# Making a block of the combined weights by pairs of row chunks with seven block products for eight

## The chip, the cores and the metric

The kernel runs on one core of one Trainium2 chip. The metric is the device time of one execution in microseconds. The core has five engines that run beside each other and meet at semaphores: TensorE (PE in the profile; its weight loads are listed apart as PEld), VectorE (DVE), ScalarE (ACT), GpSimd (POOL) and SyncE (SP), which here only issues DMAs. ScalarE and GpSimd issue DMAs too, and all DMAs run on the same 16 DMA engines.

## What is computed

Two mixture layers are applied to x of 32 batches x 128 tokens x 1024 channels, all in f32. Cut to what matters here:

```
# layer 0: every batch's channels are mixed by its own 128x128 matrix; then 64 experts, 8 per token
h = einsum('bct,bcd->bdt', x, L0_cond_weights[itok_B_1_198])
x = x + moe(h, gate_w, wg, wu, wd)
# layer 1: a linear map with a low-rank adapter per batch, then a base map with routed low-rank experts
H = x @ W.T + ((x @ A[i].T) @ Bm[i].T) * scalings[i]
x = x + (H @ base_w.T + base_b) + lora experts, whose inner maps and router also read H
```

In layer 1 everything that follows H is linear in it up to the router and the inner maps, so the kernel never makes H. It multiplies the weights instead: head = [inner maps of the lora experts (128 columns), router (8 columns), base_w.T (1024 columns)], 1160 columns in all, and the combined weights are W.T @ head (eight chunks of 128 rows) and Bm.T @ head (one chunk of 128 rows, the 8 adapters x 16). These nine row chunks, each a product over 1024 = 8 x 128, are what the change touches. They depend on weights alone, so they can be made at any time before the last stage.

## The kernel before

There are three stages. In the first (lines 344 to 549) a loop over the 32 batches mixes a batch's channels on TensorE (`mixed`, tiles ph), copies the result out on ScalarE (hT), turns it into token rows on VectorE (`as_rows`, hq) and stores it (`stored`, to hbuf); it makes the router's logits (`logits`, plog), takes the best eight of 64 (`topped`), the exponentials on ScalarE (`powers`) and the weights (`weights_of`), and every four batches counts the tokens of each expert (`counted`, tiles pcnt and prk). The second stage (line 578 on) goes through the 64 experts, each with 256 slots; its token rows are gathered by the counts that the first stage leaves. The third (line 882 on) applies layer 1 to pairs of batches.

The head's columns are cut into three blocks (`BLOCKS`, line 38): 0 to 388, 388 to 776, 776 to 1160. The first 136 columns, the inner maps and the router, lie in block 0; block 1 has base-map columns only. A block of one row chunk is made by `combined(n, d)` (line 465): eight matmuls of 128 x 128 by 128 x 388, summed in one PSUM bank (pcw), a ScalarE copy to SBUF (cw) and a store to cwbuf in HBM, from where the third stage reads it. For d = 8, the adapters' chunk, the copy goes to G_sb, which stays in SBUF. Block 0 is made in the first stage, one chunk behind each of batches 8, 11, 14, 17, 20, 23 and 26 and two behind the last; block 1 in the second stage's start, while the first gathers are on their way (line 812); block 2 in the third stage's start.

The left operand of these products, W.T and Bm.T, is loaded in three parts of three row chunks (`left_block`, tiles WB_a, 1.5 MB each): chunks 0 to 2 at batch 2, 3 to 5 at batch 5, 6 to 8 at batch 9. The right operand is one block of the head's columns (`head_block`, tile hw, 1.55 MB), loaded at batch 2 for block 0 and at batch 22 for block 1. The x of batch b + 6 is loaded at batch b into a ring of six buffers (`loaded_batch`). From batch 10 on one batch of x a turn is also copied from HBM to HBM (`carried`, to ybuf).

The order of the work is written out by hand: `dve`, `pe`, `act`, `pool` and `sync` (line 221) wrap the engines so that every instruction keeps its place in the program, and because that helper is at line 219, most rows of the profile carry L219 and are told apart by their tiles. DMAs issued by SP and ScalarE take turns on eight semaphores; an issue whose semaphore is still in use waits for the DMA that had it before to land.

`weight_sums` and `token_sums` (lines 610 and 622), `product` (634) and the same helpers of the later stages are the scheme that the change brings to the first stage as well: seven products of half-sized blocks in place of eight.

Of the kernel before, what the change touches and what calls it, by code (L numbers as in the profile page):

```python
# [8 lines left out]
F32 = mybir.dt.float32  # L9
# [3 lines left out]
ALU = mybir.AluOpType  # L13
# [4 lines left out]
P = 128  # L18
# [3 lines left out]
HC = H // P  # L22
# [15 lines left out]
BLOCKS = [(0, 388), (388, 776), (776, NO)]  # L38
PIECES = [(0, 126), (126, 320), (320, 512)]
BW = 388  # L40
NS = BLOCKS[1][1]
NA = NX + R
HH = HC // 2
# [3 lines left out]
NQ = P // Q  # L47
W4 = H // NQ
# [3 lines left out]
def kernel(  # L52
# [37 lines left out]
    cwbuf = dram.tile([P, HC, NS], F32, name="cwbuf")  # L90
# [86 lines left out]
    fs = fpool.enter_context(tc.tile_pool(name="fs", bufs=1))  # L177
# [10 lines left out]
    def head_block(n):  # L188
        lo, hi = BLOCKS[n]
        hw = wts.tile([P, HC * BW], F32, name=f"hw_{n}", tag="wg")  # L190
        hw = hw[:, 0 : HC * (hi - lo)].rearrange("p (j o) -> p j o", j=HC)
        sync.dma_start(hw, head_w[:, lo:hi].rearrange("(j p) o -> p j o", p=P))
        return hw
# [6 lines left out]
    def multiplied(n, d, hw, left, pool, tag, pe):  # L200
        w = BLOCKS[n][1] - BLOCKS[n][0]
        pcw = pool.tile([P, 512], F32, name=f"pcw_{n}_{d}", tag=tag)[:, 0:w]
        for j in range(HC):
            if j == HC // 2:
                yield
            pe.matmul(pcw, left[d][:, j, :], hw[:, j, :], start=(j == 0), stop=(j == HC - 1))
        yield pcw
# [5 lines left out]
    class InOrder:  # L213
# [7 lines left out]
    dve, pe, act, pool, sync = (  # L221
        InOrder(e) for e in (nc.vector, nc.tensor, nc.scalar, nc.gpsimd, nc.sync)
    )
# [121 lines left out]
    pa_big = ppool.enter_context(tc.tile_pool(name="pa_big", bufs=4, space=PSUM))  # L345
    pa_sm = ppool.enter_context(tc.tile_pool(name="pa_sm", bufs=3, space=PSUM))
    with (
# [6 lines left out]
        def loaded_batch(b):  # L354
            ws[b] = a6.tile([P, P], F32, name=f"w_{b}", tag="w_b")
            pool.indirect_dma_start(
                out=ws[b],
                out_offset=None,
                in_=cond_w,
                in_offset=bass.IndirectOffsetOnAxis(ap=cond_rows[:, b : b + 1], axis=0),  # L360
            )
            xs[b] = a6.tile([P, HC, P], F32, name=f"x_{b}", tag="x_q")
            queue = pool if 2 <= b < 6 else sync
            queue.dma_start(xs[b].rearrange("p j c -> p (j c)"), x_q[b])
# [5 lines left out]
        def mixed(b):  # L370
            hT = a2.tile([P, HC, P], F32, name=f"hT_{b}", tag="hT", bufs=4)
            x_b, w_b = xs.pop(b), ws.pop(b)
            for n in range(2):
                ph = pa_big.tile([P, HH, P], F32, name=f"ph_{b}_{n}", tag="big")
                for j in range(HH):
                    pe.matmul(ph[:, j, :], x_b[:, n * HH + j, :], w_b, start=True, stop=True)
                act.copy(hT[:, n * HH : (n + 1) * HH, :], ph)
            hTs[b] = hT


        def as_rows(b):
            hqs[b] = a2.tile([P, NQ, HC, Q], F32, name=f"hq_{b}", tag="hq", bufs=3)
            dve.transpose(
                hqs[b].rearrange("p b j c -> p j b c"),
                hTs[b].rearrange("p j (b i) -> p j b i", i=Q),
            )

        def stored(b):
            act.dma_start(
                hbuf[b * P : (b + 1) * P, :], hqs.pop(b).rearrange("p b j c -> p (b j c)")  # L390
            )

        def logits(b):
            g, t = divmod(b, GB)
            if t == 0:
                plogs[g] = pa_sm.tile([P, GB, E], F32, name=f"plog_{g}", tag="sm")
            hT = hTs[b]
            for j in range(HC):
                pe.matmul(
                    plogs[g][:, t, :],  # L400
                    hT[:, j, :],
                    gw_sb[:, j, :],
                    start=(j == 0),
                    stop=(j == HC - 1),
                )
# [59 lines left out]
        def combined(n, d):  # L465
            lo, hi = BLOCKS[n]
            halves = multiplied(n, d, hws[n], lefts, pa_big, "big", pe)
            next(halves)
            yield
            pcw = next(halves)  # L470
            if d < HC:
                cw = fs.tile([P, BW], F32, name=f"cw_{n}_{d}", tag="cw", bufs=3)[:, 0 : hi - lo]
                act.copy(cw, pcw)
                act.dma_start(cwbuf[:, d, lo:hi], cw)
            else:
                act.copy(G_sb[:, lo:hi], pcw)
            yield

        loaded_batch(0)
        gw_sb = a1.tile([P, HC, E], F32, name="gw_sb")  # L480
        sync.dma_start(gw_sb.rearrange("p j e -> p (j e)"), gate_w)
# [6 lines left out]
        dve.memset(pad[:, 0, :], float(NT))  # L488
        dve.memset(pad[:, 1, :], 0.0)

        rest = [(0, d) for d in range(HC + 1)]
        copies = iter(range(NB))

        def some_rows():
            for _ in combined(*rest.pop(0)):
                pass

        for b in range(NB):  # L500
            mixed(b)
            if b >= 1:
                as_rows(b - 1)
                stored(b - 1)
            if b >= 2:
                logits(b - 2)
            if b >= 3:
                topped(b - 3)
            g, t = divmod(b - 7, GB)
            if t == 0 and g >= 0:  # L510
                powers(g)
                weights_of(g)
            elif t == 1 and g >= 0:
                counted(g)
            if b + 6 < NB:
                loaded_batch(b + 6)
            if b == 2:
                hws = {0: head_block(0)}
                lefts = left_block("a", 0, "wd")
            if b == 5:  # L520
                lefts += left_block("a", 1, "wd")
            if b == 9:
                lefts += left_block("a", 2, "wu")
            if b == 22:
                hws[1] = head_block(1)
            if b >= 10:
                carried(next(copies), sync)
            if b in (8, 11, 14, 17, 20, 23, 26):
                some_rows()
            if b == 25:  # L530
                for buf in (hbuf, ybuf):
                    pool.dma_start(
                        buf[NT : NT + P, :].rearrange("p (n c) -> p n c", c=256),
                        zeros.unsqueeze(1).to_broadcast([P, H // 256, 256]),
                    )
                pool.dma_start(ranks[:, NB, :, :], pad)
# [3 lines left out]
        stored(NB - 1)  # L540
        topped(NB - 3)
        topped(NB - 2)
        some_rows()
        logits(NB - 1)
        topped(NB - 1)
        powers(NB // GB - 1)
        weights_of(NB // GB - 1)
        some_rows()
        counted(NB // GB - 1)
    part = {0: looked_up([0, 1, 2, 3])}  # L550
    fetched(part[0], 2 * NJ)
# [26 lines left out]
    with (  # L578
# [231 lines left out]
        mine = loaded(0)  # L810
        left, right = {}, {}
        for d in range(HC + 1):
            step = combined(1, d)
            next(step)
            if d == 1:
                batch_needs()
            elif d == 2:
                found_at_once(part[0], 0, 1)
            elif d == 3:
                found_at_once(part[0], 1, 2)  # L820
            next(step)
            if d in (2, 3):
                rows_spread(part[0])
                placed(part[0])
            if d == 2:
                xin = gathered(0)
                fetched(part[0], 2 * NJ)
            elif d == 3:
                halves = gathered(1)
                for _ in weight_sums(0, *mine[:2], right):  # L830
                    pass
                xT = columns(0, xin)
                for _ in token_sums(0, xT, left):
                    pass
            if d > 1:
                for _, b in zip(range(2), copies):
                    carried(b, act)
# [9 lines left out]
        for e in range(E):  # L847
# [14 lines left out]
            left, right = following  # L862
            x1, p1, o = down(e, h, wd_sb, downs, following if e + 1 < E else None, tokens, weights)
# [31 lines left out]
    step = c1.tile([P, HC], F32, name="step")  # L895
# [10 lines left out]
    t1, t2, t4 = (c1.tile([P, KC // 2, 512], F32, name=f"ts{k}") for k in (1, 2, 4))  # L906
# [4 lines left out]
    def map_sums(lo, hi):  # L911
# [7 lines left out]
    right = {  # L919
        1: rows_of(0)[:, :, 0, :],  # L920
        2: rows_of(1)[:, :, 0, :],
        3: rows_of(1)[:, :, 1, :],
        4: t4,
        5: t1,
        6: t2,
        7: rows_of(0)[:, :, 1, :],
    }
# [156 lines left out]
    lefts = left_block("b", 0, "wu")  # L1084
# [8 lines left out]
    first = PIECES[2][0]  # L1093
# [11 lines left out]
    for d in range(HC + 1):  # L1105
        _, pcw = multiplied(2, d, hw, lefts, pc_p, "pp", pe)
# [16 lines left out]
    sums = map_sums(first, 512)  # L1123
    next(sums)
    left = token_sums2(0, X)
# [9 lines left out]
    for q in range(NQP):  # L1135
# [18 lines left out]
        o = [c3.tile([P, H], F32, name=f"out{t}_{u}", tag=f"out{t}", bufs=2) for t in range(2)]  # L1154
        rows = [slice((2 * q + t) * P, (2 * q + t + 1) * P) for t in range(2)]
# [11 lines left out]
        p5 = summed("p5c", product2(5), bias[:, 1, :])  # L1167
# [13 lines left out]
        if more:  # L1181
            left = token_sums2(q + 1, X)
# [77 lines left out]
```

## Time and profile before

| | us |
|---|---|
| median of 3 runs | 2685.72 (2681.97 to 2685.94) |
| the profiled execution | 2684.73 |
| its span, first to last instruction | 2683.0 |
| first stage | 0 to about 193 |
| second stage's start, block 1's rows | about 196 to 245 |
| second stage, experts | to about 2440 |
| third stage | to 2683.0 |

The profile page is that of one execution. Its parts used here are the busy times by engine, the chain of work that ended last (followed back from the end of the kernel, at each step to what released it), the same chain in order of time, tables of busy time by stretch, the timeline of one engine or queue, and single tiles' instructions with the time from a DMA's issue to its landing. In the timelines and groups a row reads: engine, line, operation, output <- inputs, form, count. An f32 matmul is shown as two passes, so eight matmuls appear as x16. [...]

### The profile page before, as it was taken

Reading aid. Unit: us, or ns where it says so; the run is one execution under the profiler, and the core shown is the slowest. Engines: PE = TensorE matmul, PEld = TensorE weight load, DVE = VectorE, ACT = ScalarE, POOL = GpSimd, SP = SyncE. Lnnn points to the kernel's source line nnn. Section 1 sums busy time; section 2 is a strip of 40 time slices with the busy share of each in tenths; the row PEclk is TensorE's granted clock in tenths of the full one; section 3 lists DMA queues with packets and bytes.
Section 4 is the critical chain, followed back from the end, with each engine's and each line's share of the span. In section 5 each row is a group of like instructions: output and inputs, shape, how many; then the busy total and the mean of one; then the engine's idle time right before and its main releaser. Section 6 shows DMA issues by size and latency. Waiting matters only on the chain.

```text
span 2683.0 us, 24979 instructions
## 1 busy us (share of the span) xinstructions
PE 2653.0 (99%) x8740; PEld 1481.1 (55%) x8740; DVE 1833.5 (68%) x2986; ACT 540.4 (20%) x1142; POOL 1054.5 (39%) x852
## 2 busy tenths in 40 slices
PE   8999999999999999999999999999999999999999
PEld 7875455555555555555555555555555555554554
DVE  3445888788888888888888888888776444444442
ACT  3321222222222222222222222222222000000000
POOL 3106455555555554555546555464441100000000
PEclk9999999999999999999999999999999999999999
DMA  9869578878878788788787887887877422222210
GB/s 357 311 243 354 182 244 254 260 237 265 251 246 254 249 247 257 246 257 259 236 254 257 241 268 233 260 264 231 244 242 206 100 67 67 67 67 67 58 40 32
DMA packets 126364, 568.40 MB, mean 212 GB/s; under 512 B 22928, under 2 KB 48528, under 8 KB 100384
## 3 DMA queue, kind: packets, MB, share of 16 engines
q1 hardware_dynamic: 65344, 377.91, 40.4%
q0 software_dynamic: 52096, 158.45, 23.8%
q10 hardware_dynamic: 8800, 30.45, 2.9%
q8 instruction: 70, 1.15, 0.2%
q14 instruction: 54, 0.44, 0.1%
HBM read 459.68 MB, written 123.83 MB: 217 GB/s over the span
## 4 chain that ended last, share of the span: by engine, by line
PE 95%; DMA 2%; DVE 1%; POOL 1%; issue 1%; SPq 0%; ACT 0%; POOLq 0%; DVEq 0%
PE px L219 26%; PE pr_c L219 18%; PE pv L219 12%; PE py L219 6%; PE pcw L219 4%; PE plog L219 2%; PE ph L219 2%; PE pth L219 2%; DMA rkg<-ranks,row 1%; PE prk L219 1%; DMA WB_b<-in_WB 0%; DMA xin<-hbuf,slot_row 0%; POOL rkg L255 0%; DMA x<-in_x_q 0%; SPq L219 0%
## 5 line engine op out<-in xcount | busy, mean ns | idle before, releaser
L331 POOL DMA_INDIRECT xin<-hbuf,slot_row x512 | 617.1, 1205 | 171.0 <-issue 150.5
L867 POOL DMA_INDIRECT ybuf<-o,slot_tok x128 | 209.0, 1633 | 686.4 <-DVE o L219 210.5
L219 PE MATMUL pr_c<-BM,X 128*128 128x512 f32 x480 | 213.7, 592 | 0.0
L219 POOL DMA_INDIRECT ab<-in_AT,adapter_rows x32 | 38.2, 1193 | 423.8 <-ACT pxw L219 418.3
L255 POOL DMA_INDIRECT rkg<-ranks,row x128 | 153.4, 1199 | 95.5 <-DVE own L219 52.4
L219 PE MATMUL px<-wg,xT 128*128 128x384 f32 x512 | 187.4, 489 | 0.0
L219 PE MATMUL pv<-t,s 128*128 128x384 f32 x512 | 175.7, 486 | 0.0
L219 PE MATMUL px<-t,s 128*128 128x384 f32 x512 | 175.6, 486 | 0.0
L219 PE MATMUL py<-wg,xT 128*128 128x384 f32 x512 | 175.6, 486 | 0.0
L219 PE MATMUL px<-wu,xT 128*128 128x384 f32 x512 | 175.6, 486 | 0.0
L219 PE MATMUL pv<-wu,s 128*128 128x384 f32 x512 | 175.6, 486 | 0.0
L219 PE MATMUL px<-t,xT 128*128 128x384 f32 x512 | 175.6, 486 | 0.0
L219 DVE TENSOR_TENSOR t<-wu,wg 128x1536 f32<-128x1536 f32 x64 | 113.4, 1771 | 74.9 <-PE pv L219 74.7
L219 DVE STREAM_TRANSPOSE xT<-xin 128x1024 f32<-128x1024 f32 x128 | 151.8, 1223 | 4.8 <-DMA xin<-hbuf,slot_row 4.6
L219 ACT COPY u<-px 128x384 f32<-128x384 f32 x128 | 61.3, 479 | 434.0 <-PE px L219 434.0
L219 PEld LDWEIGHTS pr_c<-BM,X 128*128 128x128 f32 x480 | 88.9, 190 | 100.2 <-issue 100.0
L219 PE MATMUL pr_c<-ts,ss 128*128 128x512 f32 x320 | 142.4, 592 | 0.0
L219 PEld LDWEIGHTS pv<-t,s 128*128 128x128 f32 x512 | 97.2, 190 | 81.0 <-issue 26.3
L219 PEld LDWEIGHTS px<-t,s 128*128 128x128 f32 x512 | 97.3, 190 | 67.8
L219 PEld LDWEIGHTS py<-wg,xT 128*128 128x128 f32 x512 | 97.3, 190 | 67.8
L219 PEld LDWEIGHTS px<-wu,xT 128*128 128x128 f32 x512 | 97.3, 190 | 67.8
L219 PEld LDWEIGHTS px<-t,xT 128*128 128x128 f32 x512 | 97.3, 190 | 67.8
(1519 smaller groups left out, 4479.6 us busy)
## 6 DMA issues: line engine op xcount, KB each, us to landing
wd<-in_wd SPq DMA_DIRECT2D x64, 1536.0 KB, 8.4
wg<-in_wg SPq DMA_DIRECT2D x63, 1536.0 KB, 8.0
wu<-in_wu SPq DMA_DIRECT2D x63, 1536.0 KB, 10.3
hbuf<-hq ACTq DMA_DIRECT2D x32, 512.0 KB, 7.5
xq<-ybuf SPq DMA_DIRECT2D x64, 256.0 KB, 5.1
out_y<-out_c SPq DMA_DIRECT2D x32, 512.0 KB, 2.7
x<-in_x_q SPq DMA_DIRECT2D x28, 512.0 KB, 7.7
ybuf<-in_x SPq DMA_DIRECT2D x22, 512.0 KB, 8.5
```

The lines of the kernel that those rows point to most:

```text
L219: return lambda *args, **kw: kept(op(*args, **kw))
L255: nc.gpsimd.indirect_dma_start(out=some["rk"][:, s, :, :].rearrange("p i t -> p (i t)"), out_offset=None, in_=ranks.rearrange("e b i t -> ...
L331: nc.gpsimd.indirect_dma_start(out=xin[:, q, :], out_offset=None, in_=quarters, in_offset=bass.IndirectOffsetOnAxis(ap=slot_row[:, s : s + ...
L867: nc.gpsimd.indirect_dma_start(out=ybuf, out_offset=bass.IndirectOffsetOnAxis(ap=slot_tok[:, s : s + 1], axis=0), in_=o[j], in_offset=None ...
```

## The change

Blocks 0 and 1 change places: the first stage makes block 1, the second stage's start block 0. In the first stage the adapters' chunk (d = 8) is made first, behind batch 11, by `combined` as before. Chunks 0 to 7 are made in four pairs: a pair's two chunks, the two halves of the 1024 summed channels and the two halves of the 388 columns give 2 x 2 x 2 blocks, whose eight block products are replaced by seven, of sums of blocks (`pair_of_rows`). The sums of the right operand are made once (`block_sums`, behind row 8, one of them in place in hw), those of the left operand for each pair (`row_sums`, behind batches 12, 17, 22 and 27). The pairs stand behind batches 14, 19 and 24 and in the stage's end, where the last one is cut in two around the last batch's logits. A pair's products are summed in three PSUM buffers: x collects products 1, 6, 7 and 4 with a ScalarE copy after each, y holds product 2, v products 5 and 3; three VectorE additions finish the two chunks. The sums use buffers that stand empty in the first stage (tags xin, rkg and hit). `left_block` for chunks 6 to 8 stays at batch 9.

```diff
@@ -476,6 +476,78 @@
                 act.copy(G_sb[:, lo:hi], pcw)
             yield
+        first, end = BLOCKS[1]
+        half = (end - first) // 2
+        def block_sums():
+            b = hws[1].rearrange("p (k j) o -> p k j o", k=2)
+            b11, b12 = b[:, 0, :, 0:half], b[:, 0, :, half : 2 * half]
+            b21, b22 = b[:, 1, :, 0:half], b[:, 1, :, half : 2 * half]
+            t1, t2, t4 = (
+                fs.tile([P, NQ, W4], F32, name=f"tc{k}", tag="xin", bufs=4)
+                .rearrange("p q w -> p (q w)")[:, 0 : HH * half]
+                .rearrange("p (j o) -> p j o", j=HH)
+                for k in (1, 2, 4)
+            )
+            dve.tensor_tensor(t1, b12, b11, ALU.subtract)
+            dve.tensor_tensor(t2, b22, t1, ALU.subtract)
+            dve.tensor_tensor(b12, b22, b12, ALU.subtract)
+            dve.tensor_tensor(t4, b21, t2, ALU.subtract)
+            return {1: b11, 2: b21, 3: b22, 4: t4, 5: t1, 6: t2, 7: b12}
+        def row_sums(c):
+            a11, a12 = lefts[2 * c][:, 0:HH, :], lefts[2 * c][:, HH:HC, :]
+            a21, a22 = lefts[2 * c + 1][:, 0:HH, :], lefts[2 * c + 1][:, HH:HC, :]
+            sc = fs.tile([P, 4, HH, P], F32, name=f"sc_{c}", tag="rkg")
+            s1, s2, s3, s4 = (sc[:, k] for k in range(4))
+            dve.tensor_tensor(s1, a21, a22, ALU.add)
+            dve.tensor_tensor(s2, s1, a11, ALU.subtract)
+            dve.tensor_tensor(s3, a11, a21, ALU.subtract)
+            dve.tensor_tensor(s4, a12, s2, ALU.subtract)
+            return {1: a11, 2: a12, 3: s4, 4: a22, 5: s1, 6: s2, 7: s3}
+        def pair_of_rows(c, left, right):
+            def term(into, k, start=False, stop=False):
+                for j in range(HH):
+                    pe.matmul(
+                        into,
+                        left[k][:, j, :],
+                        right[k][:, j, :],
+                        start=(start and j == 0),
+                        stop=(stop and j == HH - 1),
+                        skip_group_check=True,
+                    )
+            x, y, v = (
+                pa_big.tile([P, 512], F32, name=f"pc{k}_{c}", tag="big")[:, 0:half] for k in "xyv"
+            )
+            cw = [
+                fs.tile([P, BW], F32, name=f"cw_1_{2 * c + i}", tag="cw", bufs=3) for i in range(2)
+            ]
+            p5 = fs.tile([P, half], F32, name=f"pc5_{c}", tag="hit")
+            lo, hi = slice(0, half), slice(half, 2 * half)
+            term(x, 1, start=True)
+            act.copy(cw[0][:, lo], x)
+            term(y, 2, start=True, stop=True)
+            term(x, 6)
+            act.copy(cw[0][:, hi], x)
+            yield
+            term(v, 5, start=True)
+            act.copy(p5, v)
+            term(x, 7)
+            act.copy(cw[1][:, hi], x)
+            term(v, 3, stop=True)
+            term(x, 4, stop=True)
+            act.copy(cw[1][:, lo], x)
+            dve.tensor_tensor(cw[0][:, lo], cw[0][:, lo], y, ALU.add)
+            dve.tensor_tensor(cw[1][:, hi], cw[1][:, hi], p5, ALU.add)
+            dve.tensor_tensor(cw[0][:, hi], cw[0][:, hi], v, ALU.add)
+            for i in range(2):
+                act.dma_start(cwbuf[:, 2 * c + i, first:end], cw[i])
+            yield
         loaded_batch(0)
         gw_sb = a1.tile([P, HC, E], F32, name="gw_sb")
         sync.dma_start(gw_sb.rearrange("p j e -> p (j e)"), gate_w)
@@ -488,12 +560,8 @@
         dve.memset(pad[:, 0, :], float(NT))
         dve.memset(pad[:, 1, :], 0.0)
-        rest = [(0, d) for d in range(HC + 1)]
         copies = iter(range(NB))
-        def some_rows():
-            for _ in combined(*rest.pop(0)):
-                pass
+        pairs = iter(range(HC // 2))
@@ -515,18 +583,26 @@
             if b + 6 < NB:
                 loaded_batch(b + 6)
             if b == 2:
-                hws = {0: head_block(0)}
+                hws = {1: head_block(1)}
                 lefts = left_block("a", 0, "wd")
             if b == 5:
                 lefts += left_block("a", 1, "wd")
             if b == 9:
                 lefts += left_block("a", 2, "wu")
             if b == 22:
-                hws[1] = head_block(1)
+                hws[0] = head_block(0)
             if b >= 10:
                 carried(next(copies), sync)
-            if b in (8, 11, 14, 17, 20, 23, 26):
-                some_rows()
+            if b == 11:
+                for _ in combined(1, HC):
+                    pass
+                sums = block_sums()
+            if b in (12, 17, 22, 27):
+                c = next(pairs)
+                rows = row_sums(c)
+            if b in (14, 19, 24):
+                for _ in pair_of_rows(c, rows, sums):
+                    pass
             if b == 25:
                 for buf in (hbuf, ybuf):
                     pool.dma_start(
@@ -540,12 +616,14 @@
         stored(NB - 1)
         topped(NB - 3)
         topped(NB - 2)
-        some_rows()
+        last = pair_of_rows(c, rows, sums)
+        next(last)
         logits(NB - 1)
         topped(NB - 1)
         powers(NB // GB - 1)
         weights_of(NB // GB - 1)
-        some_rows()
+        for _ in last:
+            pass
         counted(NB // GB - 1)
     part = {0: looked_up([0, 1, 2, 3])}
     fetched(part[0], 2 * NJ)
@@ -810,7 +888,7 @@
         mine = loaded(0)
         left, right = {}, {}
         for d in range(HC + 1):
-            step = combined(1, d)
+            step = combined(0, d)
             next(step)
             if d == 1:
                 batch_needs()
```

## The prediction

> **What bounds the kernel now.** First the page's head: busy shares and the chain that ended last.
>
> ```profile
> span 2683.0 us, 24979 instructions
> PE 2653.0 (99%) x8740; PEld 1481.1 (55%) x8740; DVE 1833.5 (68%) x2986; ACT 540.4 (20%) x1142; POOL 1054.5 (39%) x852
> PE 95%; DMA 2%; DVE 1%; POOL 1%; issue 1%; SPq 0%; ACT 0%; POOLq 0%; DVEq 0%
> ```
>
> TensorE carries 95% of the chain, so a microsecond taken from it, or an idle one added to it, reaches the end unless something else was late there already. The change sits in the first stage, so next I read that stage's part of the chain in order of time (start, duration, what).
>
> ```profile
> 40.78 2.37 PE prk L219 x12
> 43.15 5.21 PE pcw L219 x16
> 48.36 1.78 PE ph L219 x16
> 50.15 1.73 PE plog L219 x16
> ...
> 57.29 1.73 PE plog L219 x16
> 59.03 5.27 PE pcw L219 x16
> 64.30 1.78 PE ph L219 x16
> ```
>
> No gap: TensorE is the bound here. An f32 matmul shows as two passes, so the 8 matmuls of one row chunk (pcw) are x16. 43.15 is the row behind batch 8, 59.03 the row behind batch 11; batches 9, 10 and 11 fill the 10.67 us between 48.36 and 59.03. Then the same stretches by engine: which other resource is full? (Columns: busy time of PE, PEld, DVE, ACT, POOL, then granted clock, DMA share, GB/s.)
>
> ```profile
> 26.00:43.00 17.00, 17.00 (x143) 15.62 (x143) 9.76 (x27) 6.20 (x13) 3.77 (x4) 1.00 1.03 408
> 43.00:65.00 22.00, 22.00 (x137) 17.65 (x137) 7.54 (x19) 5.89 (x13) 2.83 (x3) 1.00 1.03 420
> 65.00:175.00 110.00, 110.00 (x779) 92.23 (x777) 43.68 (x122) 35.19 (x74) 15.35 (x17) 1.00 0.87 323
> ```
>
> The DMA engines are saturated from 26 to 65 us (share 1.03, 408 to 420 GB/s): TensorE is fed only because its loads were issued early. VectorE and ScalarE have room (about 40% and 30% busy). Last, the load that the moved row needs: the third part of the left operand WB_a, in SP's queue.
>
> ```profile
> 31.58 0.33 SPq L219 DMA_DIRECT2D WB_a<-in_WB  x1
> 42.59 9.50 SPq L219 DMA_DIRECT2D x<-in_x_q  x4
> 52.15 0.47 SPq L219 DMA_DIRECT2D WB_a<-in_WB  x1
> DMA to landing us min/median/max: 13.0/13.0/13.0
> ```
>
> The last line belongs to the issue at 52.15 alone: it lands at 65.1 us.
>
> **The change, part by part.** *Removed:* eight of the nine row chunks. One costs 16 passes; 5.21 us / 16 = 0.326 us a pass of 388 columns. The stage's nine rows are 46.9 us.
>
> *Added:* four pairs of 7 products x 4 matmuls x 2 passes = 56 passes of 194 columns. No pass of that width is in the trace. The nearest is 152 columns wide (px in the last stage, same chain):
>
> ```profile
> 2446.36 4.13 PE px L219 x32
> ```
>
> That is 129 ns a pass. Interpolated to 388 columns (326 ns): 129 + 42/236 x 197 = 164 ns. Bounds: 163 (half of 326) and 190 (the mean duration of a weight load, if loads were the limit); 129 ns with a 128-column load before every pass says that they are not, so 164. Pairs: 224 x 0.164 = 36.7 us. With row 8, kept whole (5.2), the stage's combined weights take 42.0 us in place of 46.9: **-5.0 us**, if TensorE never waits. Seven eighths of eight rows would be 36.5, so halving the width costs only 0.2.
>
> *Moved:* row 8 (the adapter rows, to G_sb) goes from the stage's last row to its first, behind batch 11, and the row behind batch 8 is gone. Row 8 reads WB_a's third part, which the old kernel first needs behind batch 20. Its load is still issued at batch 9. In SP's queue it stands behind x of batch 15, and that issue waits for the landing of WB_a's second part (it reuses its semaphore; 31.58 + 20.1 = 51.7). Neither depends on how far TensorE is, so I expect the issue near 52 us again. Ahead of it four x loads of 512 KB are pending or just issued.
>
> When does TensorE reach row 8? Up to 43.15 nothing is different. Then batch 9 follows at once; its x lands at about 43.8 (issued 27.84, 15.9 to landing), a wait of 0.6. Batches 9 to 11 take 10.67: TensorE stands before row 8 at 43.15 + 0.6 + 10.67 = 54.4. The data lands at 65.1 and TensorE starts 0.15 later: **10.9 us idle**. TensorE runs in written order, so batch 12 and all behind it stand too. On ScalarE the copy to G_sb is queued there with batch 12's hT copies behind it; on VectorE the in-place difference of the block (which must not overwrite what row 8 reads) with batch 11's transpose behind it. SP issues x of batches 16 and 17 and then waits for batch 12. All of them wait for TensorE, so this adds nothing.
>
> The landing is the main unknown. Its bytes are the same: one 194 KB cwbuf store fewer ahead of it, batch stores earlier by 4 to 5 us. Lower bound: if the DMA engines served nothing but SP's own queue, the last quarter of x 12, x 13 to 15 and this load, some 3.4 MB at 420 GB/s, take 8.1 us: 60.3. Upper: the slowest WB_a load took 20.1: 72.2. I take the load's own 13.0.
>
> *The clock.* What an idle TensorE costs afterwards the trace shows at the second stage's start (same columns).
>
> ```profile
> 260.00:264.00 4.00, 3.44 (x11) 1.71 (x9) 1.26 (x2) 0.10 (x1) 3.09 (x4) 1.00 1.04 375
> 264.00:268.00 4.00, 0.00 (x0) 0.00 (x0) 3.93 (x4) 0.00 (x0) 2.65 (x3) 0.98 0.92 372
> 268.00:270.00 2.00, 0.00 (x0) 0.00 (x0) 2.00 (x5) 1.27 (x3) 0.00 (x0) 0.50 0.43 166
> 272.00:274.00 2.00, 2.00 (x4) 1.01 (x3) 1.83 (x9) 0.38 (x1) 0.00 (x0) 0.50 0.00 0
> 274.00:276.00 2.00, 2.00 (x6) 0.96 (x5) 1.97 (x4) 0.50 (x1) 0.00 (x0) 0.84 0.00 0
> ```
>
> TensorE stops near 263.4, is granted 0.50 from 268 on, starts again at 270.96, and has the full clock back within 274 to 276 (0.84 is a mix: 0.64 us at half): 3.7 us worked at half speed, 1.85 lost. An idle of 10.9 is longer. The Trainium skill, "TensorE: Matmul & The Clock Gate", Part 1, speaks against this change too: after an idle window of 3.4 us the clock is halved, and it needs one busy window, at a phase that varies from run to run, to come back. From one to two windows at half speed lose 1.7 to 3.4 us. Row 1.85, rule 1.7 at least: I take **+1.7**, since a short phase is as likely as a long one (0.9 to 2.6). The sum would be 8.3 by the row, 8.2 by the rule's lower end and 6.5 with no gate.
>
> *Costed at nothing, and what hides it.* VectorE: four block differences of 776 elements (0.9 us each; 1536 take 1.77), sixteen row sums of 512 (0.69 each), twelve additions of 194 (some 0.3): about 18 us over a stage of 170 with VectorE 40% busy. The row sums are made two batches (over 7 us) before their pair. ScalarE: five 194-column copies a pair, some 0.3 us each (300 ns for 128, 483 for 388); each lies under the next product, 4 matmuls or 1.3 us. If that cover were gone, about 0.5 us a copy, up to 2.5 us a pair. PSUM: a pair takes three of four buffers; the next batch's second half needs the pair's first one back, 0.92 us after the pair ends, against 0.5 for the last copy. In the stage's end the 5.2 us of the last product half replace row 8's 5.2 over the last softmax weights, ready at 191.5 of 193.4. The later rows in stage two have the same width as before.
>
> *The sum:* -5.0 + 0.6 + 10.9 + 1.7 = **+8.2 us**. The other way round: row 8 ends at 65.3 + 5.2 + 1.7 = 72.2, where batch 12 started at 64.3; what is left is 36.7 against 36.5; +8.1. The slack cannot swallow it: stage two starts from the last batch's counts. On the profiled execution (2684.73, span 2683.0) that is 2692.9; it lies 1.0 under the median 2685.72, so on the median **2693.9 us**.
>
> **The rivals.** *No wait: the load is there in time (not slower).* One mechanism: WB_a's third part lands by 54.4. Then -5.0 + 0.6 = -4.4, or 2681.3, and at best 2680.7. For it: the issue needs only free semaphores, and would have to come some 11 us earlier. Against it: its predecessor's landing at 51.7. The change turns into a loss from a landing near 57 (65.1 less 8.2), or 58.6 if the short idle then leaves the clock alone. *A shorter wait:* landing at 58 to 62 gives -1 to +5, 2685 to 2691; the saturated stretch speaks against it. *Waits inside the pairs:* 0.5 us for each of 20 copies, or a pair's end on PSUM, adds 4 to 10: 2698 to 2704; ScalarE's 30% speaks against it. *The weight load limits 194-column passes:* 224 x 26 ns = 5.8 more, 2699.7; the 129 ns row speaks against it.
>
> **How the numbers follow.** Long wait 0.70 (2689 to 2698: landing from 62 to 66, clock loss from 0.9 to 2.6, and 1 to 2 for runs); shorter wait 0.12; no wait 0.10; additional waits or slow passes 0.08. Runs of this kernel differ by 4 us, so 0.2%, 5.4 us, is about what can be told from no change. Even the full gain of 5.0 is inside that, so no wait gives 0.05 faster and 0.05 same; the shorter wait is same; the rest is slower: 0.05, 0.17, 0.78. The range 2686 to 2699 takes in most of the shorter wait and the start of the last case.
>
> **What would show it.** Right: TensorE idle by 9 to 12 us ahead of pcw near 54 us, released by the DMA of WB_a; granted clock 0.5 in a stretch there; 194-column passes 164 ns apart; the batches behind pair one without gaps; the stage's end (pcnt, 193.4 now) near 201.6. Wrong: pcw starting by 58 us (load issued earlier), or passes near 190 ns, or gaps after each ScalarE copy in a pair.

## The result and the profile after

| | before | after |
|---|---|---|
| median of 7 runs each, us | 2685.72 (2681.19 to 2687.76) | 2694.59 (2692.16 to 2703.1) |
| profiled execution / its span | 2684.73 / 2683.0 | 2696.52 / 2694.7 |
| ratio of the runs, 95% interval | | 1.0043 (1.0031 to 1.0054) |

The change makes the kernel slower: by 8.9 us between the medians, by 8.3 to 14.5 by the interval. The head of the page after:

```profile
span 2694.7 us, 25228 instructions
PE 2655.9 (99%) x8836; PEld 1497.7 (56%) x8836; DVE 1850.3 (69%) x3018; ACT 542.9 (20%) x1154; POOL 1039.8 (39%) x852
PE 95%; DMA 2%; DVE 1%; issue 1%; POOL 0%; ACT 0%; ACTq 0%; DVEq 0%; SPq 0%
```

TensorE is the bound as before, and shown busy 2.9 us more though it does 5 us less of products: passes at half clock last longer and count as busy. Where the time went shows in the first stage. The timeline of TensorE, then the chain, around row 8 (pcw):

```profile
52.81 1.90 PE L219 MATMUL plog<-gw_sb,hT 128*128 128x64 f32 x16
66.29 7.13 PE L219 MATMUL pcw<-hw,WB_a 128*128 128x388 f32 x12 [11.59 <-issue]
```

```profile
66.29 8.43 PE pcw L219 x16
74.72 1.78 PE ph L219 x16
...
88.19 1.37 PE pcx L219 x8
89.56 1.31 PE pcy L219 x8
90.88 1.32 PE pcx L219 x8
```

TensorE has nothing to do for 11.59 us ahead of row 8, whose 16 passes then take 8.43 us; the row behind batch 8 took 5.21. Batch 12 starts at 74.72; before, at 64.30. ("issue" says that the records name no releaser; the experiments do.) Eight passes of 194 columns take 1.31 us, 164 ns a pass.

A wait in brackets counts from the end that the timeline draws for the pass before. That end lies 0.16 us too late: a pass of 388 columns is drawn 489 ns long though the next starts after 326, one of 194 is drawn 327 long though the next starts after 164. What a wait costs is counted between starts in the text below, so that 11.59 in brackets is 11.8 us lost. The same stretches by engine (busy PE, PEld, DVE, ACT, POOL, granted clock, DMA share, GB/s):

```profile
43.00:54.50 11.50, 10.85 (x97) 10.73 (x96) 4.71 (x11) 4.09 (x7) 2.82 (x3) 1.00 1.02 415
54.50:66.20 11.70, 0.20 (x2) 0.06 (x1) 3.81 (x9) 0.93 (x4) 0.00 (x0) 0.68 1.04 426
66.20:72.30 6.10, 6.01 (x10) 3.25 (x11) 0.46 (x1) 0.00 (x0) 0.00 (x0) 0.50 0.40 167
188.00:199.00 11.00, 10.26 (x52) 7.51 (x52) 5.36 (x19) 2.67 (x7) 0.00 (x0) 0.69 0.24 86
```

While TensorE stands, the DMA engines are full (1.04). The clock drops in the wait, and the first 6 us of work run at half. A second drop, near 190 us, was not forecast. Nor was this wait, in the third pair (2.0 us between starts); first TensorE, then the chain that leads to it, then ScalarE:

```profile
151.95 1.48 PE L219 MATMUL pcy<-hw,WB_a 128*128 128x194 f32 x8
155.24 1.58 PE L219 MATMUL pcx<-tc,sc 128*128 128x194 f32 x8 [1.81 <-ACT cw L219]
```

```profile
139.47 14.82 DMA hw<-in_head_w
154.29 0.02 issue
154.31 0.02 ACTq L219
154.33 0.04 issue
154.37 0.45 ACTq L219
154.82 0.04 issue
154.86 0.33 ACT cw L219
155.19 0.04 issue
155.24 1.58 PE pcx L219 x8
```

```profile
154.37 0.45 ACTq L219 DMA_DIRECT2D ranks<-rk  x1
154.86 0.32 ACT L219 COPY cw<-pcx 128x194 f32<-128x194 f32 x1 [3.45 <-DMA hw<-in_head_w]
```

ScalarE has to issue a store of ranks before it copies the pair's first sum out of PSUM. That issue waits for a semaphore which the 1.55 MB load of block 0 still holds, and product 6, which must not add to x before it is copied, waits behind both.

### The profile page after: what moved, and what is told of

It reads as the page before. It is cut to its first block, busy times and chain, and to the rows that moved or that the text cites. A ratio compares the mean times of both kernels' runs of the same rounds, so it can differ in the third digit from the quotient of the medians.

```text
span 2694.7 us, 25228 instructions
## 1 busy us (share of the span) xinstructions
PE 2655.9 (99%) x8836; PEld 1497.7 (56%) x8836; DVE 1850.3 (69%) x3018; ACT 542.9 (20%) x1154; POOL 1039.8 (39%) x852
## 4 chain that ended last, share of the span: by engine, by line
PE 95%; DMA 2%; DVE 1%; issue 1%; POOL 0%; ACT 0%; ACTq 0%; DVEq 0%; SPq 0%
PE px L219 27%; PE pr_c L219 18%; PE pv L219 12%; PE py L219 6%; PE pcw L219 3%; PE ph L219 2%; PE pth L219 2%; PE plog L219 2%; PE pcx L219 1%; PE prk L219 1%; DMA hw<-in_head_w 1%; DMA x<-in_x_q 0%; DMA hbuf<-hq 0%; PE pcv L219 0%; DMA ybuf<-in_x 0%
## 5 line engine op out<-in xcount | busy, mean ns | idle before, releaser
L331 POOL DMA_INDIRECT xin<-hbuf,slot_row x512 | 605.9, 1183 | 166.8 <-issue 155.7
L219 DVE TENSOR_TENSOR t<-wu,wg 128x1536 f32<-128x1536 f32 x64 | 113.5, 1773 | 77.3 <-PE pv L219 77.3
L219 PEld LDWEIGHTS pv<-wu,s 128*128 128x128 f32 x512 | 97.3, 190 | 67.8
```

Source lines behind the costliest of these rows:

```text
L219: return lambda *args, **kw: kept(op(*args, **kw))
L331: nc.gpsimd.indirect_dma_start(out=xin[:, q, :], out_offset=None, in_=quarters, in_offset=bass.IndirectOffsetOnAxis(ap=slot_row[:, s : s + ...
```

## The experiments

Each was measured beside the kernel before on the same chip (medians 2684.1 to 2684.4 there, with 20 to 43 runs), so the ratios are to be compared. "Stage one ends" is the last counting matmul in the run's own profile, "half clock" the time at granted clock 0.5 up to there (with TensorE idle too: 7.6 of the 20.5 us after lie in the wait), "to expert 0" the distance from there to the first expert's first transpose (pth).

| kernel | median | ratio (95%) | row 8 or first row starts | half clock | stage one ends | to expert 0 |
|---|---|---|---|---|---|---|
| before | 2685.72 | | 43.0 | 0 | 193.6 | 77.3 |
| before, again | 2683.17 (one run) | | 43.4 | 6.8 | 197.0 | 75.1 |
| after | 2694.59 | 1.0043 (1.0031 to 1.0054) | 66.3 | 20.5 | 209.4 | 73.8 |
| after, again | 2695.52 (one run) | | 67.0 | 13.7 | 206.0 | 75.5 |
| chunks 6 to 8 loaded first | 2684.24 | 1.0000 (0.9991 to 1.0010) | 56.7 | 3.4 | 193.2 | 77.6 |
| loaded later | 2699.39 | 1.0059 (1.0045 to 1.0072) | 70.9 | 27.3 | 214.7 | 78.0 |
| ordinary rows for pairs | 2697.48 | 1.0053 (1.0040 to 1.0066) | 66.5 | 17.1 | 209.5 | 73.6 |
| busy in the wait | 2693.55 | 1.0048 (1.0030 to 1.0065) | 68.3 | 10.2 | 206.3 | 74.4 |
| loaded first, block 0 later | 2686.28 | 0.9999 (0.9991 to 1.0008) | 55.6 | 10.2 | 196.9 | 75.8 |
| and row 8 behind batch 8 | 2684.13 | 0.9999 (0.9991 to 1.0007) | 42.4 | 10.2 | 194.0 | 74.7 |
| and half a pair ahead of batch 30's logits | 2682.81 | 0.9991 (0.9983 to 0.9999) | 42.4 | 6.8 | 193.1 | 75.1 |
| and pairs behind 14, 20, 27 | 2680.36 | 0.9985 (0.9977 to 0.9993) | 42.7 | 3.4 | 190.5 | 74.0 |
| before, row of batch 8 behind 29 | 2689.98 | 1.0017 (1.0009 to 1.0024) | 55.5 | 10.2 | 200.1 | 76.6 |

The last column varies by over 4 us with no order in it: 77.3 and 75.1 in two profiles of one kernel. That is why single spans are not compared below. Between the first profiles of before and after, 15.8 us at the end of stage one are 11.7 at the end of the span, and 3.5 of the 4.1 between them lie in this column.

**Chunks 6 to 8 loaded first.** The load in question early, all else in place.

```diff
             if b == 2:
...
-                lefts = left_block("a", 0, "wd")
+                third = left_block("a", 2, "wu")
             if b == 5:
-                lefts += left_block("a", 1, "wd")
+                lefts = left_block("a", 0, "wd")
             if b == 9:
-                lefts += left_block("a", 2, "wu")
+                lefts += left_block("a", 1, "wd")
+                lefts += third
```

> The changed kernel with the three parts of WB_a loaded in another order: chunks 6 to 8 at batch 2, 0 to 2 at batch 5, 3 to 5 at batch 9; bytes, places of the loads and everything on TensorE stay. Theory (row 8 waits for its load): the load lands long before row 8, no idle ahead of pcw, no half clock behind it: -5.0 for the seven products plus 0.6 for batch 9's x, 2681 us, 13 under the changed kernel; up to 2 more for the wait inside the third pair that the trace after shows. Rival (the time goes into the pairs: copies, PSUM, narrow passes): those are all still there, at most the wait moves, so 2690 or more.

Measured: 2684.24, ratio 1.0000. The chain of this run:

```profile
27.87 16.37 DMA x<-in_x_q
44.24 0.14 issue
44.38 3.65 PE ph L219 x16
...
55.18 1.73 PE plog L219 x16
56.91 5.27 PE pcw L219 x16
```

Row 8 follows the logits without a gap and takes 5.27 us: the wait and the half clock behind it are gone, and with them the loss against before (11.5 us by the ratios, 13 expected). The rival falls. The 3 us that are missing against the forecast (2681) show in the trace: batch 9's x came 1.7 us late, no row being there to cover it, and batch 9's mixing then ran at half clock (3.65 us instead of 1.84). The third pair waited 1.2.

**The same load, later.** Moved from batch 9 to 11.

```diff
-            if b == 9:
-                lefts += left_block("a", 2, "wu")
...
             if b == 11:
+                lefts += left_block("a", 2, "wu")
                 for _ in combined(1, HC):
```

> The changed kernel with the load of chunks 6 to 8 issued at batch 11 instead of 9, behind the x loads of batches 16 and 17 and two copies of x to ybuf. Theory: those four 512 KB transfers stand ahead of it in SP's queue, it lands 4 to 7 us later (70 to 73 us in the trace), the idle ahead of pcw grows by the same, the half clock stays: 2699 to 2701 us. Rival (the wait is hidden or is given back later in the stage): 2694 to 2696, as the changed kernel.

Measured: 2699.39, ratio 1.0059. Here the chain names the releaser:

```profile
59.74 11.01 DMA WB_a<-in_WB
70.75 0.14 issue
70.88 7.32 PE pcw L219 x16
```

Issued at 59.74, landed at 70.75, and pcw starts 0.14 us later, 4.6 us later than after the change. So the load sets the start of row 8, and the stage, which ends at 214.7, does not give the delay back. The time agrees (2699 to 2701 forecast), though its interval overlaps that of the changed kernel; the trace carries the proof.

**Ordinary rows in the pairs' places.** The eighth product back, everything else of the change kept.

```diff
-                sums = block_sums()
-            if b in (12, 17, 22, 27):
-                c = next(pairs)
-                rows = row_sums(c)
             if b in (14, 19, 24):
-                for _ in pair_of_rows(c, rows, sums):
-                    pass
+                c = next(pairs)
+                for d in (2 * c, 2 * c + 1):
+                    for _ in combined(1, d):
+                        pass
...
-        last = pair_of_rows(c, rows, sums)
-        next(last)
+        for _ in combined(1, HC - 2):
+            pass
...
-        for _ in last:
-            pass
+        for _ in combined(1, HC - 1):
+            pass
```

> The changed kernel with each pair replaced by its two chunks made the old way, eight matmuls of 388 columns each, at the same places; no sums, no halves; row 8 first behind batch 11 as in the changed kernel. Theory: the wait stays as it is, and the 5.0 us of the eighth product come back: 224 passes of 164 ns become 128 of 326, 36.7 to 41.7; 2699.6 us (less 2 if the third pair's wait on ScalarE goes with the pairs). Rival (the pairs lose in copies, PSUM waits and sums what they save in products): within 1.5 us of the changed kernel, or under it.

Measured: 2697.48, ratio 1.0053 against 1.0043: some 3 us over the changed kernel, with intervals that overlap. The trace is sharper. In its chain the two chunks behind batch 14 are:

```profile
88.43 10.48 PE pcw L219 x32
98.91 1.78 PE ph L219 x16
```

10.48 us for two chunks, against 88.19 to 97.45, 9.26 us, for the pair after the change: 1.22 a pair, 4.9 for four, as forecast. And this kernel has no wait behind batch 24: 4.9 less that 2.0 is the 3 us. The pairs earn what they should, save in the third. The landing ahead of row 8 is on record in this trace: issued at 53.51, 12.9 us to landing, so 66.4, and pcw starts at 66.53.

**Busy during the wait.**

```diff
             if b == 11:
+                idle = pa_big.tile([P, 512], F32, name="idle", tag="big")
+                for _ in range(12):
+                    pe.matmul(idle, ones, gw_sb.rearrange("p j e -> p (j e)"), start=True, stop=True)
                 for _ in combined(1, HC):
```

> The changed kernel with twelve more matmuls of 128 x 128 by 128 x 512 on TensorE ahead of row 8, on data that lies in SBUF, into a PSUM bank that nobody reads: 24 passes of 0.43 us, 10.3 of the 11.7 us that TensorE idles there. They do no part of the computation. Theory (the idle costs a half clock behind it): the wait stays, the clock does not drop, row 8 takes 5.2 in place of 8.4 us: 1.7 to 3 us faster than the changed kernel, 2692 to 2693. Rival (no clock loss, the wait is all): same as the changed kernel; if the added work outlasts the wait, slower by what sticks out.

Measured: 2693.55, ratio 1.0048, no difference from the changed kernel that could be told. TensorE's timeline and its clock, then the load:

```profile
57.95 10.52 PE L219 MATMUL idle<-gw_sb,ones 128*128 128x512 f32 x24
68.30 5.38 PE L219 MATMUL pcw<-hw,WB_a 128*128 128x388 f32 x16
```

```profile
58.00:68.30 10.30, 10.30 (x25) 4.56 (x25) 3.72 (x9) 0.11 (x1) 0.00 (x0) 1.00 1.04 428
68.30:74.00 5.70, 5.70 (x22) 3.52 (x21) 2.89 (x3) 0.28 (x1) 0.00 (x0) 1.00 0.11 47
```

```profile
53.80 0.79 SPq L219 DMA_DIRECT2D WB_a<-in_WB  x1
DMA to landing us min/median/max: 12.8/12.8/12.8
```

The mechanism is there: the clock stays at 1.00 and row 8 takes 5.2 us. The time forecast (1.7 to 3 us less) did not show. The added work began only at 57.95, since batch 9 had waited 2.4 us and run at half clock; the load landed at 66.6, and row 8 could start only when the added work was through, at 68.3. Some 1.7 us of the gain went there: row 8 ends at 73.7, where it ended at 74.7 after the change.

**Block 0's load behind the third pair**, on top of the new load order.

```diff
-            if b == 22:
-                hws[0] = head_block(0)
...
             if b == 25:
+                hws[0] = head_block(0)
```

> The load order of the run with chunks 6 to 8 first, and the load of block 0 (hw, 1.55 MB) issued at batch 25, behind the third pair, instead of batch 22. Theory (the third pair waits because ScalarE, ahead of the pair's first copy, stands before a ranks store whose semaphore the hw load still holds): the gap inside the third pair goes, 1.2 to 2 us under the run with the load order alone, 2682 to 2683. Rival (that gap comes from the copies or PSUM): the gap stays, no difference.

The third pair of this run:

```profile
138.31 1.48 PE L219 MATMUL pcy<-hw,WB_a 128*128 128x194 f32 x8
139.62 1.48 PE L219 MATMUL pcx<-tc,sc 128*128 128x194 f32 x8
```

Product 6 starts 1.31 us behind product 2: no gap, so the explanation of that wait holds. The time did not follow: 2686.28, ratio 0.9999, where 2682 to 2683 was forecast. The profile has 10.2 us of half clock at the end of stage one instead, from 177.0 on, and just ahead of it a wait that is new. First the chain, then VectorE and TensorE at batch 30's logits:

```profile
162.80 11.68 DMA hbuf<-hq
```

```profile
174.58 1.25 DVE L219 STREAM_TRANSPOSE hq<-hT 128x1024 f32<-128x1024 f32 x1 [4.45 <-DMA hbuf<-hq]
176.42 3.08 PE L219 MATMUL plog<-gw_sb,hT 128*128 128x64 f32 x16 [2.29 <-DVE left L219]
```

A store to hbuf takes 11.68 us to land, VectorE waits for it, and the logits wait for VectorE: 2.29 us, against 0.74 in the run with the load order alone. Block 0's load, the only thing moved between these two runs, went out at 149.15 here and at 126.93 there. So the move took the load out of the third pair's way and probably into that of the stores at the stage's end; with one profile of each, that is argued, not shown.

**Row 8 behind batch 8**, on top of that (the block's sums go there too).

```diff
-                lefts += left_block("a", 1, "wd")
-                lefts += third
+                lefts[3:6] = left_block("a", 1, "wd")
...
-            if b == 11:
+            if b == 8:
+                lefts += [None] * 3 + third
                 for _ in combined(1, HC):
```

> Chunks 6 to 8 loaded first, block 0 at batch 25, and row 8 behind batch 8 instead of batch 11, so that TensorE has a row's work there again while batch 9's x is on its way. Theory: no wait ahead of batch 9, none ahead of row 8, none in the third pair, no half clock at 44 us: the full 5.0 us of the seven products, 0.18% under the kernel before (2680.7 on its median of 2685.7, 2679 on 2684). Rival (the stage cannot be faster, the loads bind it, or stage two's start takes the gain back): within 1.5 us of the kernel before.

Measured: 2684.13, ratio 0.9999; the forecast of 5 us less fails. All three waits are gone, yet stage one ends at 194.0. The new wait ahead of batch 30's logits is there again (2.40 us, VectorE waiting 4.30 for a store to hbuf), and in it the clock goes to half, from 173.2 for 10.2 us, which costs about 5. A half clock at that place is not special to the new kernels, as the next run shows; the longer wait ahead of it is.

**The kernel before, once more.**

> The kernel before once more, for a second profile. Theory: where its clock windows fall otherwise, a half clock of 3 to 10 us shows near 176 us, at the end of stage one, and that end comes 2 to 5 us later than 193.6; no wait ahead of pcw. Rival (only the changed kernels lose the clock there): end of stage one within 1 us of 193.6, full clock.

```profile
172.00:179.00 7.00, 6.25 (x55) 6.13 (x55) 2.66 (x8) 2.00 (x6) 0.00 (x0) 1.00 0.33 137
179.00:185.70 6.70, 6.70 (x18) 3.11 (x17) 3.05 (x11) 1.16 (x2) 0.00 (x0) 0.50 0.16 35
```

Clock 0.50 from 179.0 to 185.7, and stage one ends at 197.0 instead of 193.6, as forecast. The wait ahead of the logits is 0.75 here and 0.74 in the first profile, so the same work met the half clock once and not the other time.

**The changed kernel, once more.**

> The changed kernel once more, for a second profile. Theory: the wait ahead of pcw (11 to 12 us) and the half clock behind it are there again; the half clock near the end of stage one depends on where the clock's windows fall and need not be; the distance from the last counts to the first expert's transpose is 73.8 us in the trace after and 77.3 in the one before, and if that is chance of the gathers it may be either here. Rival (stage two's start is shorter in the changed kernel by what it does): 73 to 74 again.

```profile
67.00 7.37 PE L219 MATMUL pcw<-hw,WB_a 128*128 128x388 f32 x16 [12.07 <-issue]
154.79 1.58 PE L219 MATMUL pcx<-tc,sc 128*128 128x194 f32 x8 [1.71 <-ACT cw L219]
```

Between starts the wait ahead of row 8 was 12.2 us, the third pair's 1.9; row 8 took 7.37 us, 1.1 less than in the first profile. No half clock at the end of stage one, which ended at 206.0, 12.4 us behind the first profile of before, where there was none either. The distance to expert 0 was 75.5, neither 73 to 74 again nor 77.3: no sign that the changed kernel shortens it.

**The row behind batch 8 moved, in the kernel before.**

```diff
-            if b in (8, 11, 14, 17, 20, 23, 26):
+            if b in (11, 14, 17, 20, 23, 26, 29):
```

> The kernel before with one thing moved: the row behind batch 8 goes behind batch 29 (rows behind 11, 14, 17, 20, 23, 26 and 29). Same work. Theory (that row covered the wait for batch 9's x): a gap of 0.6 to 2.5 us ahead of batch 9, with up to 1.7 more where the clock drops to half: 1 to 4 us slower than the kernel before. Rival (the x loads catch up, nothing is lost): same as the kernel before.

Measured: 2689.98, ratio 1.0017 (4.6 us, a little over the forecast's 1 to 4). TensorE's timeline:

```profile
44.72 2.02 PE L219 MATMUL ph<-w,x 128*128 128x128 f32 x16 [1.68 <-DMA x<-in_x_q]
```

Taking that row away opens 1.68 us ahead of batch 9. The clock kept 1.00 there in this profile, and went to 0.5 for 10.2 us at the stage's end. The gap is shown; how the remaining 3 us divide between the two places is not.

**Half a pair ahead of batch 30's logits; then the pairs later.** The first diff is on top of row 8 behind batch 8, the second on top of the first.

```diff
+        last = pair_of_rows(c, rows, sums)
+        next(last)
         logits(NB - 2)
         counted(NB // GB - 2)
...
         topped(NB - 2)
-        last = pair_of_rows(c, rows, sums)
-        next(last)
```

```diff
-            if b in (12, 17, 22, 27):
+            if b in (12, 17, 22, 28):
...
-            if b in (14, 19, 24):
+            if b in (14, 20, 27):
```

> The run with row 8 behind batch 8, with the first half of the last pair moved from behind to ahead of batch 30's logits at the stage's end. Theory (a clock window of 3.4 us in which TensorE's array works less than some 0.36 of the time halves the clock, and the sparse stretch of logits, wait and counts in the stage's end falls under that in some executions; 10 us at half lost 5 in that run's trace): the 0.9 us wait ahead of those logits is filled with dense products, no half clock near 175 us, and the gain of about 5 us shows: 2679 to 2680 on a kernel before of 2684. Rival (the gain is taken back in stage two's start): 2683 to 2685, with the end of stage one near 188 us all the same.

> The same as the run before it with the pairs behind batches 14, 20 and 27 instead of 14, 19 and 24, so that the last batches have dense work nearer to them. Theory of the clock windows: as that run, or up to 1 us better if a half clock is left there; rival: same as the kernel before.

Measured: 2682.81 (0.9991) and 2680.36 (0.9985, interval 0.9977 to 0.9993). The first gained 2.4 us of the 5 forecast, and its clock still went to half, from 182.9 for 6.8 us. It has a wait inside the half pair that was moved:

```profile
175.31 1.58 PE L219 MATMUL pcx<-tc,sc 128*128 128x194 f32 x8 [1.04 <-ACT cw L219]
```

Ahead of that copy ScalarE had the softmax exponentials, which waited 3.65 us for VectorE, and VectorE 4.12 us for a store to hbuf, as in the two runs before. The second gained more than forecast. It is 4 us faster than the kernel before and about 15 faster than the changed one, by the ratios. Its first stage in stretches, as the prediction showed those of before:

```profile
43.00:65.00 22.00, 22.00 (x158) 18.50 (x157) 13.73 (x33) 7.14 (x15) 3.77 (x4) 1.00 1.03 418
65.00:175.00 110.00, 110.00 (x853) 104.48 (x854) 56.29 (x146) 36.34 (x83) 14.70 (x16) 1.00 0.86 330
175.00:190.00 15.00, 14.05 (x83) 12.48 (x82) 6.34 (x23) 3.04 (x9) 0.00 (x0) 0.89 0.18 54
```

No gap until 175; the half clock that is left lasts 3.4 us. But two things changed at once: with a pair fewer ahead of batch 25, block 0's load goes out at 137.72 instead of 146.60, and the wait for the store to hbuf is gone from TensorE's way. How much of the gain is the earlier load and how much the dense work near the last batches, no run separates.

## Why the prediction was right, point by point

The time (2693.9 forecast, 2694.59 measured) and its reason, row 8 in front of a load that has not landed, both hold: with the load early the loss is gone, with the load later it grows. The closeness of the time is in part luck, as the terms show.

- *Products, -5.0.* Right: 164 ns a pass, 1.22 us a pair less.
- *Batch 9's x, 0.6.* 0.8 in the profile after (0.65 in brackets, released by that DMA), but 1.3 to 2.4 in the others without a row there, with a half clock behind it in four. Mis-sized: the row behind batch 8 covered more than one trace showed.
- *The wait, 10.9.* 11.8 and 12.2 in two profiles. The load was issued at 53.0, where I had it near 52, and pcw started at 66.3, where I had 65.3. That the issue follows the landing of WB_a's second part holds in every trace that gives both: 0.4 to 0.5 us behind it before (52.15) and in three runs (52.41, 53.51, 53.80).
- *The clock, 1.7.* Taken at its low end: row 8 took 8.43 and 7.37 us instead of 5.22, so 3.2 and 2.2; of the work behind the wait, the first 6.0 and 3.9 us ran at half.
- *Costed at nothing: ScalarE's copies in the pairs.* This step failed. I set the copies' 0.3 us against the 1.3 us of the next product and asked whether ScalarE is busy; what held it was a DMA issue ahead of the copy in its queue, waiting for another transfer's semaphore. 1.9 to 2.0 us in one of four pairs.
- *Stage one's end, 201.6.* It came at 209.4 in the profile and at 206.0 in the second one. Take the second one's own terms: to the 8.2 us add 1.7 for row 8's later start (67.0 against 65.3), 0.5 for the clock and 1.9 for the third pair. That makes 12.3, against 12.4 measured between the two profiles without a half clock at the stage's end. The first profile has that half clock (some 3 us) on top.
- *"The slack cannot swallow it."* No run here shows that stage two's start gives anything back for a reason; it varies by 4 us, and a single pair of profiles can hide as much.

So the sum was some 4 us short at the end of stage one. The medians, at 8.9, look nearer to it than the ratio's 1.0043 (11.5 us) and the traces allow: that nearness is luck.

Of the rivals, the weight load as limit of narrow passes is excluded by 164 ns, the load in time and the shorter wait by the gap of 11.6 us. Waits inside the pairs were partly true, once instead of in every copy.

## What to carry to other kernels

When work is moved earlier in a written order, look first at which load it reads and at when that load lands in the trace, not at where its issue stands in the program; the work left behind may have been the cover of another load. For each copy that "fits under the next product", look also at what stands ahead of it in that engine's queue, DMA issues and their semaphores included. When a load is moved out of one wait's way, look at what it meets in its new place: here, it seems, the stores at the stage's end. A saving of a few microseconds on TensorE can be lost to the clock, as in the run with row 8 behind batch 8: look at the granted clock, stretch by stretch, before believing or doubting a small difference.

## What the runs showed of the hardware

TensorE's clock did not need an idle window to drop. All stretches at clock 0.5 that end inside a trace last 3.413 us or a multiple of it (3.41, 6.83, 10.24, 13.65), and their edges lie on one grid of 3.413 us in each trace, whose phase differs from run to run. For each window of that grid, from 41 us on in all thirteen traces (some 10,000), I added up the array time of its passes. It is an estimate: columns x 0.83 ns, the slope between 152 columns (129 ns) and 388 (326 ns), and twice that at half clock.

| share of the window that the array worked | what the next window was granted |
|---|---|
| at full clock, 0.00 to 0.37 (48 windows) | half |
| 0.38 and more (all others) | full |
| at half clock, up to 0.73 | half |
| 0.75 and 0.76 (one each) | full, half |
| 0.79 and more | full |

The two windows nearest to the line at full clock have 0.373 and 0.379, closer than the estimate is good for. The share for which TensorE is shown busy draws no such line: windows with up to 0.78 of it were followed by half, and one with 0.47 by full.

The Trainium skill ("TensorE: Matmul & The Clock Gate", Part 1) has the window of 3.4 us, free-running, and the two states; it names an idle window as the cause. Here windows with TensorE at work through most of them dropped the clock too: the logits' passes of 64 columns stand 112 ns apart and work the array for 53 by the same estimate, so a window of such passes, with 0.9 us of waiting in it, falls under 0.37. Whether that happens depends on where the grid lies. In the first profile of before, the window from 175.67 us has 0.405 and the clock stays; in the second, the window from 175.53 has 0.373 and the clock goes to half. That fits the end of stage one at 193.6 and at 197.0. That the dense products near the last batches won, in the last kernel, by raising this share is argued from these windows and one profile, beside the earlier load named above; the half clock was not switched off by itself.
